# A graph layer on one core: bin counts in PSUM, an earlier rank chain and a new order of the edge phase

## The chip, the cores and the metric

One Trainium2 chip, one core. The metric is the time of the kernel on the device in microseconds (us); where several runs are given, their median. Five engines work side by side: TensorE (PE in the rows, PEld for its weight loads), VectorE (DVE), ScalarE (ACT), GpSimd (POOL) and SyncE (SP, which here issues the plain transfers). Sixteen DMA engines move the data.

## What is computed

A graph layer over 3,327 nodes with 1,024 features, float32. Every node has itself and some 16 others as neighbours (adjacency of int32, density 0.0024 made symmetric, with a full diagonal).

```
h = relu(layernorm(x))
f = h @ Wf + bf
g = h @ Wg + bg
e = relu(f @ g.T)
attention = softmax(where(adj > 0, e, -9e15), axis=1)
out = x + attention @ (h @ W + bW)
```

## The kernel before

The kernel does not form the 3,327 x 3,327 scores. It finds each node's list of neighbours, sorts the nodes by their number of neighbours, and gathers for each node only the rows of its neighbours. (Where a list doesn't fit the layout, a flag sends the kernel to a dense path; with these inputs it isn't taken.) The product A = Wf Wg^T is formed once, so that a node's q = h A + bias and its score with a neighbour is the dot of q with the neighbour's h.

**The loop** (`for i in range(NT - 3)`, 26 tiles of 128 nodes, 23 iterations). SP loads a tile of adjacency, 1.66 MB, into one of five key buffers `r` (`load_adj(i + 5)`, L682, behind the tile that frees the buffer). ScalarE makes ones of the entries and sums them (`degrees`, L699). GpSimd multiplies them by the column number, in two halves (`keys`, L706). VectorE takes the eight largest of each of 16 segments (`segments`, L770 and L772), and out of these 128 candidates the 24 largest as the list (`listed`, L783 to L787; L779 counts the candidates for a later comparison with the degree). Between them stand the layer norm of x (`measured` either on VectorE, L715 and L717, or on ScalarE, L729 and L732; `rooted`, L724, L725 or L733; `inverted`, L737; `scaled`, L742 and L743; `store_h`, L747, to the table `hd` in DRAM), the stores of the lists into the tail of `hd`'s rows (`store_lists`, L757) and of the leftover candidates (`store_left`, L752, into `cd`), and on TensorE the transposes and products that make A (L826, L842, emptied by ScalarE, L846).

**The rank.** Nodes are put in order of their degree, in 48 bins. `one_hot` (L795) marks each node's bin. TensorE sums the one-hots over the nodes ahead: `before(t)` (L803) adds tile t's with an upper triangle, `after(t)` (L806) the rest with a lower one, in one running PSUM tile `pre`; between the two VectorE reads `pre` and keeps each node's place in its bin (`placed`, L811, into `rp`). This alternation goes on through the loop.

**The bridge**, behind the loop: the last tiles are normalised and listed (24 is `late`, 25 is `last`), a scan over the bins (L1040), a multiplication with the one-hots (L1041) and a reduction (L1051) give the rank, L1053 to L1083 turn it into two one-hot matrices (`ohp` by comparison with `iotaq`, a pattern that GpSimd writes, L937), and 26 matmuls (L1087) give `perm`, the order of the nodes (L1101). Then the rows of the first two tiles of the order are gathered from `hd` (L641), transposed, and their q is made in thirds (L1117, emptied at L1137). SP loads the eight parts of W (L996) between the stores.

**The edge phase.** For each of the 26 tiles in the new order: gathers of its own rows (H, `G<-hd,perm`), of the leftovers (C, first tile only) and of each neighbour (G, `G<-hd,G`) on GpSimd (L641), dots on VectorE (`junk`, L1271), the softmax, weighted sums of rows on VectorE (L1324) or on ScalarE and TensorE (L1307, L1311), the next tiles' q on TensorE (L1258), the product with W (L1339), the addition of x by a gather that accumulates, and a scatter. F (L1236 to L1239) makes the first tile's longer list out of the leftovers. All engines run in a static order, which a planner in the file works out when the kernel is built: `steps_of` lists the steps with durations and dependences, `FREE_AT` says when each engine is free to begin, `planned` improves the ranks in `PASSES` rounds with random changes from `SEED`, and the best order found is emitted.

## Time and profile before

| | us |
|---|---|
| median of three runs | 1209.29 (1203.59 to 1210.39) |
| the profiled execution | 1202.4 |
| its span in the trace | 1200.7 |
| TensorE busy | 1092.0 (91%) |
| VectorE busy | 1118.7 (93%) |
| GpSimd busy | 897.1 (75%) |
| ScalarE busy | 606.6 (51%) |

The span is cut in three here: the loop, to about 190 us; the bridge, to about 250; the edge phase, to the end. Busy shares over the whole span mix these three, so the rows below are read by stretch. A timeline row gives the start, the duration, the engine, the line of the code, the operation with its output and inputs, how many there are, and in brackets how long the engine had been idle and who released it.

### The profile page before, as it was taken

How to read it: one execution, taken by the hardware profiler on the slowest of the kernel's cores; microseconds unless marked ns; L12 is line 12 of the kernel's file. 1: busy time of each engine (PE TensorE's matmuls, PEld its weight loads, DVE VectorE, ACT ScalarE, POOL GpSimd, SP SyncE). 2: the span in 40 equal slices, each digit the busy share in tenths (PEclk: the TensorE clock that was granted, in tenths of full speed). 3: DMA queues.
4: the chain of work that ended last, by engine and by line, in shares of the span. 5: the costliest groups of instructions: out<-in, count | busy, mean ns of one | idle time of the engine just before them, and what ended most of it. 6: DMA issues, size and time to landing. Idle time of an engine off the chain costs nothing.

```text
span 1200.7 us, 13971 instructions
## 1 busy us (share of the span) xinstructions
PE 1092.0 (91%) x4508; PEld 696.3 (58%) x4508; DVE 1118.7 (93%) x2209; ACT 606.6 (51%) x925; POOL 897.1 (75%) x627
## 2 busy tenths in 40 slices
PE   2799992699968999999999999999999999999997
PEld 2566661367537567566665666665556656555553
DVE  5999999869998999999999999999999999999982
ACT  6799887427418446535554354444433433333251
POOL 8999999178777888777877788768767777777711
PEclk9799996799988999999999999999999999999999
DMA  9999999699978999997999889889989888898932
GB/s 369 418 406 395 393 376 307 228 346 330 329 228 308 315 310 322 331 327 264 328 330 304 292 282 309 302 269 296 307 280 306 264 287 284 290 309 256 300 105 55
DMA packets 98408, 361.98 MB, mean 301 GB/s; under 512 B 14857, under 2 KB 18184, under 8 KB 95125
## 3 DMA queue, kind: packets, MB, share of 16 engines
q0 software_dynamic: 75264, 274.11, 68.9%
q1 hardware_dynamic: 23060, 86.87, 19.0%
q8 instruction: 37, 0.61, 0.2%
q14 instruction: 47, 0.39, 0.1%
HBM read 331.46 MB, written 29.49 MB: 301 GB/s over the span
## 4 chain that ended last, share of the span: by engine, by line
DVE 37%; PE 28%; DMA 12%; issue 11%; POOL 7%; ACT 4%; SPq 0%; POOLq 0%; DVEq 0%; ACTq 0%
DVE junk L1271 16%; DVE G L1324 13%; PE p_o L1339 11%; PE p_q L1258 8%; PE p_y L1311 6%; DMA G<-hd,G 5%; POOL r L706 4%; DVE cand L772 3%; POOL G L641 2%; PE ps_A L1117 2%; DMA G<-hd,perm 2%; ACT G L1307 2%; DMA A_sb<-in_L_gnn_Wg_dram 1%; DMA hd<-pay 1%; DMA xt<-in_x_dram 1%
## 5 line engine op out<-in xcount | busy, mean ns | idle before, releaser
L641 POOL DMA_INDIRECT G<-hd,G x430 | 557.9, 1297 | 167.5 <-issue 94.5
L1271 DVE CUSTOM_DVE_ANT_0 junk<-G,q 128x1024 uint8<-128x1024 f32 x468 | 562.1, 1222 | 14.3 <-DMA G<-hd,G 9.4
L1339 PE MATMUL p_o<-W_sb,yT 128*128 128x512 f32 x832 | 367.2, 593 | 3.5 <-ACT yT L1335 3.3
L1324 DVE SCALAR_TENSOR_TENSOR G<-G,sc 128x1024 f32<-128x1024 f32 (+1 forms) x281 | 354.4, 1262 | 5.3 <-ACT G L1296 4.3
L1258 PE MATMUL p_q<-A_sb,hT 128*128 128x342 f32 x1152 | 345.6, 451 | 2.0 <-ACT p_q L1267 1.5
L1258 PEld LDWEIGHTS p_q<-A_sb,hT 128*128 128x128 f32 x1152 | 212.9, 190 | 106.7 <-issue 7.4
L1339 PEld LDWEIGHTS p_o<-W_sb,yT 128*128 128x128 f32 x832 | 154.3, 189 | 182.7 <-issue 174.1
L1311 PEld LDWEIGHTS p_y<-ident,G 128*128 128x128 f32 x1552 | 176.2, 142 | 38.4 <-issue 19.6
L1311 PE MATMUL p_y<-ident,G 128*128 128x128 f32 x1552 | 188.9, 275 | 5.3 <-ACT G L1307 3.7
L706 POOL TENSOR_TENSOR r<-r,iotaj 128x1664 f32<-128x1664 f32 (+3 forms) x50 | 183.8, 3718 | 5.0 <-ACT r L699 5.0
L1307 ACT ACTIVATE G<-G,sc 128x1024 f32<-128x1024 f32 x168 | 178.8, 1138 | 0.1
L842 PE MATMUL ps_A<-WgT,WfT 128*128 128x342 f32 x432 | 129.3, 458 | 1.8 <-ACT WfT L837 1.8
L772 DVE MAX8 cand<-r 128x8 f32<-128x208 f32 (+2 forms) x416 | 119.2, 360 | 1.3 <-POOL r L706 1.0
L1264 ACT COPY q<-p_q 128x342 f32<-128x342 f32 x72 | 31.8, 441 | 156.7 <-PE p_q L1258 148.1
L1350 ACT ACTIVATE xp<-p_o,unit 128x512 f32<-128x512 f32 x50 | 34.1, 685 | 142.3 <-PE p_o L1339 116.8
L842 PEld LDWEIGHTS ps_A<-WgT,WfT 128*128 128x128 f32 x432 | 81.1, 191 | 41.7 <-ACT WfT L837 2.0
L699 ACT ACTIVATE r<-r 128x3327 f32<-128x3327 int32 (+3 forms) x27 | 77.3, 2863 | 10.0 <-DMA r<-in_adj_dram 7.2
L1335 ACT COPY yT<-p_y 128x512 f32<-128x512 f32 x52 | 30.1, 585 | 86.3 <-PE p_y L1311 86.0
L641 POOL DMA_INDIRECT xp<-in_x_dram,perm x25 | 46.4, 1856 | 27.0 <-ACT xp L1350 20.0
L1357 POOL DMA_INDIRECT out_dram<-xp,perm x25 | 31.8, 1273 | 40.9 <-DMA xp<-in_x_dram,perm 37.5
L1292 ACT ACTIVATE sc<-sc,unit 128x10 f32<-128x10 f32 (+10 forms) x36 | 11.0, 305 | 78.4 <-DVE unit L1282 51.4
L641 POOL DMA_INDIRECT G<-hd,perm x26 | 36.8, 1417 | 18.2 <-DVE ne L1165 9.3
(149 smaller groups left out, 689.0 us busy)
## 6 DMA issues: line engine op xcount, KB each, us to landing
r<-in_adj_dram SPq DMA_DIRECT2D x24, 1663.5 KB, 11.1
xt<-in_x_dram SPq DMA_DIRECT2D x22, 512.0 KB, 12.2
hd<-xt SPq DMA_DIRECT2D x22, 512.0 KB, 10.6
G<-hd,G POOLq DMA_INDIRECT x430
A_sb<-in_L_gnn_Wg_dram SPq DMA_DIRECT2D x8, 512.0 KB, 17.2
A_sb<-in_L_gnn_Wf_dram SPq DMA_DIRECT2D x8, 512.0 KB, 11.8
W_sb<-in_L_gnn_W_dram SPq DMA_DIRECT2D x8, 512.0 KB, 7.7
cd<-cand SPq DMA_DIRECT2D x25, 64.0 KB, 11.5
```

What stands on the lines that cost most here:

```text
L641: return nc.gpsimd.indirect_dma_start(out=to, out_offset=None, in_=table, in_offset=bass.IndirectOffsetOnAxis(ap=idx, axis=0), **kw,)
L699: nc.scalar.activation(r[:n, b:e], a[:n, b:e], AF.Sign, accum_out=to)
L706: eng.tensor_mul(r[:n, b:e], r[:n, b:e], iotaj[:n, b:e])
L772: nc.vector.max(cands[t][:n, s * 8 : s * 8 + 8], r[:n, s * SW : min(N, (s + 1) * SW)])
L842: nc.tensor.matmul(ps[:, :QB], WfTs[c][:, k, :], WgT[:, k, o : o + QB], start=(k == 0), stop=(k == KD - 1))
L1258: nc.tensor.matmul(ps_q[(3 * t + i) % 2][:, :QB], hT[:, k, :], A_sb[:, k, i * QB : (i + 1) * QB], start=False, stop=(k == KD - 1), skip_gr ...
L1271: nc.vector.tensor_tensor_reduce(junks[k % 2], row(t, k), q[:, :D], 1.0, 0.0, op0=ALU.mult, op1=ALU.add, accum_out=scs[t % 3][:, k : k + 1],)
L1307: nc.scalar.activation(g, g, AF.Copy, scale=scs[t % 3][:, k : k + 1])
L1311: nc.tensor.matmul(ps_y[g][:, c, :], of[:, (4 * g + c) * P : (4 * g + c + 1) * P], ident, is_transpose=True, start=((t, g) not in begun an ...
L1324: nc.vector.scalar_tensor_tensor(y, row_k, scs[t % 3][:, k : k + 1], y, op0=ALU.mult, op1=ALU.add)
L1339: nc.tensor.matmul(ps_o[o], yT[:, k, :], W_sb[:, k, o * CB : (o + 1) * CB], start=False, stop=(k == KD - 1), skip_group_check=True,)
L1350: nc.scalar.activation(to, ps_o[o], AF.Copy, scale=rss[t % 3])
```

## The change

Bin counts. `before`, `after` and `placed` leave the loop. `counted(t)`, for all tiles in one go behind the loop, adds tile t's one-hots into every later tile's 48 columns, in three PSUM banks of ten, ten and six tiles, with a matrix of ones; a tile's own 48 columns get the triangle, and `pre` the total. VectorE then subtracts the banks from the scan, multiplies by the one-hots and reduces: that is the rank.

Order of the bridge. The steps of the rank come first on VectorE; the segments and the list of tile 23 and several measurements come behind `perm`. The two halves of `iotaq` are written once at the start by ScalarE, into the buffers that later hold q, so GpSimd's pattern (L937) goes. The first tile's rows are gathered from x as soon as `perm` is there, and normalised anew; the second tile's still come from `hd`. All parts of W are loaded ahead of that gather, where before two of them came at the end of the bridge.

Check of lists. The count of candidates in `listed` goes; instead the entries of four finished lists are counted at once, and F of the first tile counts its longer list. The matmul that gathers the flag becomes a step of the planner (`ws`).

Planner. New starting times, 40 passes for 30, seed 5 for 3, F longer. All orders of the edge phase are therefore new.

The diff, cut to its core (`...` where lines are left out):

```diff
@@ planner
-PASSES = 30
-SEED = 3
+PASSES = 40
+SEED = 5
-FREE_AT = {"POOL": 238.1, "PE": 266.1, "ACT": 265.3, "DVE": 245.0, "DMA": 238.0}
+FREE_AT = {"POOL": 235.0, "PE": 254.0, "ACT": 253.5, "DVE": 239.0, "DMA": 235.0}
-            add("DVE", 1.8, 1.9, ("F", t), ("Cd", t), frees=[("C", t)])
+            add("DVE", 2.8, 2.9, ("F", t), ("Cd", t), ("Hd", t), frees=[("C", t)])
-                    ("M", t), at=(249.4, 263.2)[t] if t < 2 else 0.0,
+                    ("M", t), at=(240.0, 251.5)[t] if t < 2 else 0.0,
...
@@ listed
-            nc.vector.tensor_scalar(
-                pos[:n], cand[:n], 0.0, None, op0=ALU.is_gt, op1=ALU.add, accum_out=cnt[:n, t : t + 1]
-            )
...
+                some = pos[:n, : (u + 1) * KL]
+                nc.vector.tensor_scalar(some, held[:n, NBIN : NBIN + (u + 1) * KL], 0.0, None, op0=ALU.is_gt)
+                nc.vector.tensor_reduce(
+                    cnt[:n, t - u : t + 1], some.rearrange("p (t k) -> p t k", k=KL), AX.X, ALU.add
+                )
...
+        def counted(t):
+            for b in range(t // RB, -(-NT // RB)):
+                t0, t1 = max(b * RB, t + 1), min((b + 1) * RB, NT)
+                if t1 > t0:
+                    nc.tensor.matmul(
+                        banks[b][:, t0 * NBIN - b * RB * NBIN : (t1 - b * RB) * NBIN], ones,
+                        oh[:, t, None, :].to_broadcast([P, t1 - t0, NBIN]), start=(t == 0), stop=False, skip_group_check=True,
+                    )
+                if b == t // RB:
+                    nc.tensor.matmul(
+                        banks[b][:, (t - b * RB) * NBIN : (t + 1 - b * RB) * NBIN], tri, oh[:, t, :], start=False,
+                        stop=(t + 1 == t1), skip_group_check=True,
+                    )
+            nc.tensor.matmul(pre, ones, oh[:, t, :], start=(t == 0), stop=(t == NT - 1), skip_group_check=True)
...
+            qs = [qpool.tile([P, QW], FP, name="q") for s in ORDER[:2]]
+            HP = P // 2
+            iotaq = [q.bitcast(BF)[:, : HP * NT].rearrange("p (d t) -> p d t", t=NT) for q in qs]
+            for i, to in enumerate(iotaq):
+                nc.scalar.copy(to, iotap[:, i * HP : (i + 1) * HP, None].to_broadcast([P, HP, NT]))
...
@@ behind the loop
             measured(19, True)
             rooted(19)
             inverted(18)
-            s = 0
-            after(counted - 1)
-            for t in range(counted, NT):
-                before(t)
-                segments(NT - 3, s, s + 4)
-                s += 4
-                placed(t)
-                after(t)
...
+            one_hot(last, NT)
+            banks = [p_mm.tile([P, CB], FP, name="ps_A") for _ in range(-(-NT // RB))]
+            for t in range(NT):
+                counted(t)
...
-            nc.vector.tensor_mul(above, oh, incl[:, None, :].to_broadcast([P, NT, NBIN]))
+            for b, ps in enumerate(banks):
+                t0, t1 = b * RB, min((b + 1) * RB, NT)
+                nc.vector.tensor_tensor(
+                    above[:, t0:t1, :], incl[:, None, :].to_broadcast([P, t1 - t0, NBIN]),
+                    ps[:, : (t1 - t0) * NBIN].rearrange("p (t d) -> p t d", d=NBIN), op=ALU.subtract,
+                )
...
-            hps = []
-            for s in ORDER[:2]:
-                hps.append(ln.tile([P, D], FP, name="xt"))
-                gather(hps[-1], hd, perm[:, s : s + 1])
+            load_W(6)
+            load_W(7)
+            hps = [ln.tile([P, D], FP, name="xt")]
+            xs[first] = hps[0]
+            gather(hps[0], x[:, :], perm[:, ORDER[0] : ORDER[0] + 1])
+            measured(late, False)
+            rooted(late)
+            segments(NT - 3, 0, SEG)
+            inverted(late)
+            scaled(late)
+            store_h(late)
+            measured(first, True)
+            rooted(first)
+            measured(last, True)
+            inverted(first)
+            scaled(first)
+            rooted(last)
...
@@ F
+            some, number, due = (G[buf["C", t]][:, i : i + w] for i, w in ((SEG * 8, KX + 8), (D - 2, 1), (D - 1, 1)))
+            nc.vector.tensor_scalar(some, found, 0.0, None, op0=ALU.is_gt, op1=ALU.add, accum_out=number)
+            degree = told(t).bitcast(FP)[:, KL : KL + 1]
+            nc.vector.tensor_scalar(due, degree, 7.0 - KL, 0.0, op0=ALU.add, op1=ALU.max)
+            nc.vector.tensor_tensor(due, due, number, op=ALU.not_equal)
+            nc.vector.tensor_tensor(worst, worst, due, op=ALU.max)
```

The order of the instructions at three places, as the engines get them. VectorE in the loop, before: the count and the list of tile 21, the rank sums, four tiles' one-hots and the segments of tile 22 (`r` are the keys, `cand` the candidates, `held` the lists, `hit,rp` the rank sum).

```order
L779 TENSOR_SCALAR held,cnt<-cand 128x128
L783 MAX held<-cand 128x8
L785 MATCH_REPLACE cand<-held,cand 128x128
L783 MAX held<-cand 128x8
L785 MATCH_REPLACE cand<-held,cand 128x128
L783 MAX held<-cand 128x8
L811 SCALAR_TENSOR_TENSOR hit,rp<-pre,oh 128x48 x2
L795 TENSOR_TENSOR oh<-held,pay 128x192
L772 MAX cand<-r 128x8 x8
L737 RECIPROCAL rstd<-rstd 128x1
L770 TENSOR_TENSOR r<-r,held 128x128
```

Two rank sums and the count stand between one tile's candidates and the next tile's segments.

The same place after.

```order
L779 MAX held<-cand 128x8
L781 MATCH_REPLACE cand<-held,cand 128x128
L779 MAX held<-cand 128x8
L781 MATCH_REPLACE cand<-held,cand 128x128
L779 MAX held<-cand 128x8
L796 TENSOR_TENSOR oh<-held,pay 128x192
L771 MAX cand<-r 128x8 x8
L736 RECIPROCAL rstd<-rstd 128x1
L769 TENSOR_TENSOR r<-r,held 128x128
L771 MAX cand<-r 128x8 x8
```

The count ahead of the list and the two rank sums behind it are gone; one-hots and segments follow the list at once.

VectorE in the bridge up to `perm`, before: the comparison that gives `ohp`, the list of tile 23 with its count, `perm`, and the segments of tile 24 (`tens` is the rank's product in PSUM).

```order
L1083 TENSOR_TENSOR r<-lob,iotaq 128x3328
L737 RECIPROCAL rstd<-rstd 128x1
L737 RECIPROCAL rstd<-rstd 127x1
L779 TENSOR_SCALAR held,cnt<-cand 128x128
L783 MAX held<-cand 128x8
L785 MATCH_REPLACE cand<-held,cand 128x128
L783 MAX held<-cand 128x8
L785 MATCH_REPLACE cand<-held,cand 128x128
L783 MAX held<-cand 128x8
L787 TENSOR_SCALAR pay<-held 128x4x24
L1099 COPY tens<-ps_A 128x26
L1100 SCALAR_TENSOR_TENSOR tens<-ps_A,tens 128x26
```

A whole list stands between `ohp` and `perm`.

The same place after, from the last place product.

```order
L1058 TENSOR_SCALAR r<-r,part_no 128x26x26
L736 RECIPROCAL rstd<-rstd 128x1
L714 BN_STATS st<-r 128x6 x2
L716 BN_AGGR mv<-st 128x2
L714 BN_STATS st<-xt 128x6 x2
L716 BN_AGGR mv<-st 128x2
L1074 COPY tens<-ps_A 128x26
L1075 SCALAR_TENSOR_TENSOR tens<-ps_A,tens 128x26
L1076 TENSOR_SCALAR perm<-tens 128x26
L736 RECIPROCAL rstd<-rstd 128x1 x2
L769 TENSOR_TENSOR r<-r,held 128x128
L771 MAX cand<-r 128x8 x16
```

The list has moved behind `perm`, two measurements stand in its stead, and the segments that follow are those of tile 23, which before stood ahead of the scan.

GpSimd from the last keys to the first neighbours, before (`xt<-hd,perm` is the gather for the first q's, `G<-hd,perm` is H).

```order
L706 TENSOR_TENSOR r<-r,iotaj 127x1663
L937 IOTA iotaq 128x3328
L641 DMA xt<-hd,perm 128x1024 x2
L641 DMA G<-hd,perm 128x1049 x3
L641 DMA G<-cd,perm 128x128
L641 DMA G<-hd,G 128x1024 x26
```

Both gathers for the first q's read `hd`, behind the pattern.

The same place after.

```order
L705 TENSOR_TENSOR r<-r,iotaj 127x1664
L705 TENSOR_TENSOR r<-r,iotaj 127x1663
L641 DMA xt<-in_x_dram,perm 128x1024
L641 DMA xt<-hd,perm 128x1024
L641 DMA G<-hd,perm 128x1049 x3
L641 DMA G<-cd,perm 128x128
L641 DMA G<-hd,G 128x1024 x26
```

The pattern is gone and the first of the two gathers reads x; the gathers behind them are in the same order here.

## Rows read from the trace of the kernel before

**Rows 1.** Windows: each engine's busy us (count), granted clock, DMA share, GB/s.
```profile
50.00:100.00 50.00, 48.99 (x201) 32.99 (x200) 47.47 (x195) 46.40 (x71) 50.00 (x15) 1.00 1.02 409
...
180.00:184.00 4.00, 4.00 (x17) 2.54 (x16) 3.96 (x15) 2.80 (x7) 3.40 (x1) 1.00 1.01 212
...
196.00:200.00 4.00, 0.24 (x2) 0.14 (x2) 2.74 (x11) 3.85 (x9) 4.00 (x2) 0.50 0.91 358
...
300.00:600.00 300.00, 276.85 (x1270) 184.59 (x1269) 289.44 (x449) 145.61 (x212) 233.31 (x174) 0.97 0.90 306
```

**Rows 2.** The chain up to 260 us, in order of time: start, us, what.
```profile
175.54 0.33 SPq L682
175.93 13.63 DMA r<-in_adj_dram
...
227.03 4.19 DMA xt<-hd,perm
```

**Rows 3.** Waits of SP (50:200) and VectorE (180:260, 250:600): total, times, longest.
```profile
SPq L682 <- DVE cand L772: 70.9, 16, 6.5
...
DVE mask L1246 <- DMA G<-hd,perm: 9.6, 3, 6.2
...
DVE junk L1271 <- DMA G<-hd,G: 9.4, 13, 1.7
```

**Rows 4.** Timeline of the loop's last tiles on GpSimd and VectorE.
```profile
165.03 14.75 POOL L706 TENSOR_TENSOR r<-r,iotaj 128x1664 f32<-128x1664 f32 x4 [0.78 <-ACT r L699]
180.59 22.01 POOL L706 TENSOR_TENSOR r<-r,iotaj 128x1664 f32<-128x1664 f32 x6 [0.81 <-ACT r L699]
...
175.51 0.29 DVE L779 TENSOR_SCALAR_CACHE_REDUCE held<-cand 128x128 f32<-128x128 f32 x1
...
177.57 0.19 DVE L811 SCALAR_TENSOR_TENSOR hit<-pre,oh 128x48 f32<-128x48 f32 x1
```

**Rows 5.** Timeline from the loop's end to perm.
```profile
180.99 4.85 PE L842 MATMUL ps_A<-WgT,WfT 128*128 128x342 f32 x16
...
189.67 2.98 ACT L699 ACTIVATE r<-r 127x3327 f32<-127x3327 int32 x1 [2.40 <-DMA r<-in_adj_dram]
...
197.41 0.28 ACT L725 ACTIVATE rstd<-mv,eps 128x1 f32<-128x1 f32 x1
...
200.62 1.04 ACT L729 ACTIVATE lnj<-r 128x1024 bf16<-128x1024 f32 x1
...
203.29 0.29 ACT L733 ACTIVATE rstd<-sums,eps 128x1 f32<-128x1 f32 x1
...
204.76 1.46 DVE L1041 TENSOR_TENSOR r<-oh,incl 128x1248 f32<-128x1248 bf16 x1
...
207.69 1.40 DVE L1051 TENSOR_REDUCE rank<-r 128x26 f32<-128x1248 f32 x1
...
216.25 1.93 PE L1087 MATMUL ps_A<-r 128*128 128x52 bf16 x26 [11.81 <-DVE r L1083]
...
221.52 0.18 DVE L1101 TENSOR_SCALAR perm<-tens 128x26 int32<-128x26 f32 x1
```

**Rows 6.** Timeline of VectorE behind perm: segments, last list.
```profile
221.81 4.51 DVE L772 MAX8 cand<-r 128x8 f32<-128x208 f32 x16
...
235.57 0.18 DVE L787 TENSOR_SCALAR pay<-held 127x24 int32<-127x24 f32 x1
```

**Rows 7.** Timeline of the first gathers, the W loads and the first q.
```profile
227.03 1.11 POOL L641 DMA_INDIRECT xt<-hd,perm  x1 [19.23 <-DVE held L779]
...
237.84 0.85 SPq L996 DMA_DIRECT2D W_sb<-in_L_gnn_W_dram  x2
...
238.73 0.94 POOL L641 DMA_INDIRECT G<-hd,perm  x1 [9.33 <-DVE ne L1165]
...
246.00 0.94 POOL L641 DMA_INDIRECT G<-hd,G  x1 [2.59 <-DMA G<-hd,perm]
...
250.89 0.45 ACT L1137 COPY q<-ps_A 128x342 f32<-128x342 f32 x1 [3.68 <-PE ps_A L1117]
```

More of the change, by code (lines that the diff above doesn't have):

```diff
@@ L607, in rows @@
     def rows(t):
[L608 removed]
+        return min(P, N - t * P) if t < NT else P
     def pieces(t):
@@ L996, in load_W @@
                 nc.sync.dma_start(W_sb[:, k, :], W[k * P : (k + 1) * P, :])
-            late, last = NT - 2, NT - 1
+            late, last, first = NT - 2, NT - 1, NT
             empty()
             load_x(last)
-            for k in range(2):
-                load_W(k)
             one_hot(late, last)
-            one_hot(last, NT)
             measured(19, True)
@@ L1021, in edge_path @@
             store_h(18)
-            scaled(19)
-            store_h(19)
-            load_W(2)
-            measured(20, False)
-            rooted(20)
-            rooted(21)
+            for k in range(2):
+                load_W(k)
             work = kpool.tile([P, N], FP, name="r")
@@ L1072, in edge_path @@
             load_W(4)
-            inverted(23)
-            scaled(23)
-            store_h(23)
-            load_W(5)
-            nc.vector.tensor_scalar(place[:, :, 1, :], ohs, part, None, op0=ALU.mult)
-            measured(last, True)
-            measured(late, False)
-            rooted(late)
-            rooted(last)
             ps = p_mm.tile([P, CB], FP, name="ps_A")
-            nc.vector.tensor_tensor(
-                ohp, lob[:, None, :].to_broadcast([P, P, NT]), iotaq, op=ALU.is_equal
-            )
             for t in range(NT):
@@ L1090, in edge_path @@
                 )
-            inverted(late)
-            scaled(late)
-            store_h(late)
-            inverted(last)
-            scaled(last)
-            store_h(last)
-            listed(NT - 3)
+            measured(21, True)
+            rooted(21)
+            measured(23, True)
+            rooted(23)
             tens = c1.tile([P, NT], FP, name="tens")
@@ L1129, in edge_path @@
             empty()
-            pq.append(bank(0, True))
-            third(pq[0], hTs[0], 0)
+            listed(NT - 3)
+            store_lists(NT - 2 - BATCH, NT - 2)
+            inverted(last)
+            scaled(last)
+            store_h(last)
+            store_left(NT - 3)
+            hps.append(ln.tile([P, D], FP, name="xt"))
+            gather(hps[1], hd, perm[:, ORDER[1] : ORDER[1] + 1])
+            pq.append(bank(0, True))
+            for i in range(3):
+                third(pq[i], hTs[0], i)
+                nc.scalar.copy(qs[0][:, i * QB : (i + 1) * QB], pq[i][:, :QB])
+                if i < 2:
+                    pq.append(bank(i + 1, False))
             transposed(hTs[1], hps[1])
             empty()
-            for j in range(6):
-                if j < 5:
-                    third(pq[j + 1], hTs[(j + 1) // 3], (j + 1) % 3)
-                nc.scalar.copy(qs[j // 3][:, j % 3 * QB : (j % 3 + 1) * QB], pq[j][:, :QB])
-                if j < 2:
-                    pq.append(bank(j + 1, False))
-            store_lists(NT - 2 - BATCH, NT - 2)
-            store_left(NT - 3)
+            for i in range(3):
+                third(pq[3 + i], hTs[1], i)
+                nc.scalar.copy(qs[1][:, i * QB : (i + 1) * QB], pq[3 + i][:, :QB])
             segments(late, 0, SEG)
@@ L1150, in edge_path @@
             store_left(last)
-            for k in range(6, KD):
-                load_W(k)
             over = c1.tile([P, 1], FP, name="over")
```

101 lines of the change are left out of this document (42 added, 59 removed).

## The prediction

> **What bounds the kernel now.** I read the page first, then the loop by windows and waits, then the stretch from the loop's end to the edge phase by the chain and the timeline. VectorE and TensorE are the busiest engines. In the loop that is not the whole story. GpSimd has no gap there (50.00 of 50 us from 50 to 100) and the DMA share stands at 1.02 [rows 1], so a lighter VectorE seems worth nothing. But SP stood on VectorE's segments (L772) for 70.9 us in 16 waits [rows 3]: it loads a tile into a buffer that VectorE has to free. The last load, of tile 25 into tile 20's buffer, goes out at 175.54, as tile 20's segments end, and lands 13.63 us after its start, at 189.56 [rows 2]. GpSimd had tile 20's keys ready before 164.3, where its idle time ahead of 165.03 begins (165.03 and 180.59 start four and six half-tile multiplications, tiles 21, 22 and then 23 to 25 [rows 4]). A tile's segments take 4.8 us (0.28 and 4.51 [rows 6]), so VectorE began tile 20's at 170.7: it lags by 6.4 us. And while the last tile's load runs, the share is still 1.01 but the rate is 212 GB/s, against 409 in the loop [rows 1]: the engines count as busy with little to do.
>
> Behind the loop the bridge is a chain of VectorE, ScalarE and TensorE steps. perm is ready at 221.70, the last list at 235.75, the first gather of the edge phase (H of the first tile) starts at 238.73, the first gather of neighbours at 246.00, the first tile's q is complete at 251.34 [rows 5 to 7]. After that the dots wait for neighbours' rows (9.4 us in 13 waits from 250 to 600 [rows 3]); apart from these VectorE is the bound, with 289.44 of 300 us busy from 300 to 600 [rows 1].
>
> **1, the loop.** Per tile VectorE loses the candidate count (0.29 and its read-out of 0.14, overlapping) and the rank sum (0.19 and 0.08) [rows 4], some 0.6 us; the list check that comes in is two small instructions in four tiles, by like rows 0.45, 0.1 a tile. 0.5 us by some twenty tiles is 10 us, more than the lag of 6.4, so VectorE follows the keys closely at the end and tile 25's load is issued 5 to 6 us earlier. What that does to its landing has two ends: nothing, if the share of 1.02 means a full queue; 6.4, if the load meets free capacity. I take -5.0, since the 212 GB/s row is nearer to the second. All that ScalarE does behind tile 25's degrees moves along: it had waited 2.40 us for that load [rows 5].
>
> **2, the rank.** In the times of before: the last one-hot now stands behind inverted(18), whose input ScalarE finishes at 197.7 [rows 5]. With the shift, 192.7. The 26 tiles' counts are 105 matmuls of 18,096 columns in all, which start when TensorE's last product ends (185.84 in before [rows 5]; 184 here, since the waits for the rank sums go). By the f32 row of 16 matmuls of 342 columns in 4.85 us they take 16.0; by half of what 26 matmuls took at a granted clock of 0.50 (1.93, so 37 ns each) 3.9 [rows 5]. They end at 188 to 200. Wanted are 193.2, and 1.5 us behind it are slack (below), so the cost is 0 to 5.4; I take 0. [...]
>
> Then scan 0.25, subtraction from PSUM in three pieces (1,248 elements, by the 1.46 us multiplication of that size 1.5 to 1.8), multiplication 1.46 and reduction 1.40 [rows 5]: 198.2. The reciprocal for tile 20 stands ahead of the next step. Its input comes from ScalarE, which behind the subtraction (195.1) scales tile 19 (some 1.6) and measures tile 20 in 2.96, as from 200.62 to 203.58 before [rows 5]: 199.6. Then 0.6 for four small steps, 0.85 + 0.86 + 0.38 for the place products, 1.9 for the two halves of the comparison: 204.3. The 26 matmuls (1.93) lie under two measurements of 1.48 on VectorE: 207.3, and **perm at 207.9**, 13.8 us earlier than 221.70. Of these 5.0 are the loop's, 4.8 the segments of tile 23, which now come behind perm, 1.5 a measurement and 2.5 the lists; the rest are waits.
>
> **3, VectorE behind perm.** Segments of tile 23 (4.8, [rows 6]) to 212.7; a wait for ScalarE's measurement of tile 24 to 214.4; measurements of the first and last tile 2.9; lists of 23 with their check 2.7, to 220.1; segments and lists of 24 and 25, by rows 4.8 and 2.1 to 2.4 each, to **233.9** against 235.75 [rows 6]. The stores and the wait that follow took 2.98 us; so **H at 236.9**, 1.8 earlier. Two W loads of 512 KB stood in the queue ahead of it, at 237.84 [rows 7]; in the new program they are issued before the first gather. From H to the first neighbours' gather were 7.27 us; an undisturbed gather landed in 4.19 [rows 2]. I take 5.2, between: **neighbours from 242.1**, 3.9 earlier. The bounds from the two durations are -1.8 and -4.9.
>
> **4, the first q.** The first tile's rows come from x at 208.1 and wait for no store of normalised rows; before, that gather stood 19.23 us and went at 227.03 [rows 7]. Landing 212.3, measured on VectorE to 215.9, scaled at 218.9, then some 19 us for transposes and three thirds of 4.85 (the first at the lower clock): q at 237.9, 13.4 earlier, and the second three thirds of 4.7 and a gather's wait later, at 253.4. This is not what counts: the first dot waits for H's rows (241), the following for the neighbours. VectorE's 9.6 us of waits for these rows [rows 3] also cover the extra 0.9 us of the four new steps in F; without that cover they would cost that.
>
> **5, the edge phase.** The amount of work is the same, but the planner starts from other times, another seed and more passes, so all of the static order is new. Its price does not show in any row of before. VectorE waited 9.4 us for neighbours' rows between 250 and 600, in 13 waits [rows 3]; a new order could save about half, -5, or double them, +9. The planner assumes GpSimd free at 235.0 and TensorE at 254.0; I get 236.9 and about 256, two later each, and an order made for earlier times makes someone wait: +2.
>
> **The sum.** -3.9 + 2 = -1.9 us on the profiled execution's 1202.4, so 1200.5. The median of the runs shown is 1209.29, 6.9 above that execution; against it the forecast is **1207.4 us**. Half a per cent, about what a measurement of this kernel can tell from no change, is 6 us: bounds 1203.2 and 1215.3.
>
> **Rivals.**
> *The order and the early q carry through* (faster). TensorE has made q 13 us earlier and the order is made for that; if the 9.4 us of waits are halved and neighbours come at the early end: -4.9 - 4.7 = -9.6, 1199.7. For it: TensorE and ScalarE enter the edge phase with a lead. Against: VectorE is 96% busy from 300 to 600 and its work is not less. Chance 0.22.
> *The loop ends where it did* (no change). The load of tile 25 lands at 189.56 again, because the queue is full. For it: 1.02. Against: 212 GB/s. Then -3.9 + 5.0 + 2 = +3.1, 1212.4. Chance 0.20.
> *The counts are slow* (slower). TensorE's granted clock was 0.50 from 196 to 200, with TensorE nearly idle [rows 1]. If the counts run at that level and at the 74 ns per 52 columns of the bf16 row, 18,096 columns take 25.8 us and end at 209.8 instead of 194.7: +15.1. It decides as soon as they take over 10.7 us. Sum +13.2, 1222.5. Against: TensorE comes from full work, with products up to 185.84, and works on without a break. Chance 0.07.
> *The order fits badly* (slower). The waits of 250 to 600 double: -3.9 + 9.4 = +5.5, and with neighbours at the late end +7.6, 1214.8 to 1216.9. Chance 0.11.
> The forecast itself (1204 to 1211) has 0.40.
>
> **How the numbers follow.** Faster than 1203.2: nearly all of the first rival and a tenth of the forecast, 0.25. Slower than 1215.3: the slow counts, most of the bad order, and the upper tail of the unmoved loop, 0.17. Within: 0.58. The range leaves out the slow counts and the far ends: 1198 to 1217.
>
> **What would show it.** Step 1: the last adjacency load issued near 170 and landed near 184 or 185. Step 2: matmuls of the counts without gaps, done by 194, perm near 208. Step 3: H near 237, neighbours from 242. Step 4: q near 238 and 253, first dot not waiting for q. Step 5: VectorE's waits from 250 to 600 near 10 us. The forecast is wrong if the last load lands at 189 again, if the counts run past 196, or if VectorE's waits after 300 differ by over 5 us from before.

## The result, and the profile after

The changed kernel takes 1213.07 us in the median of 20 runs, the kernel before, run beside it, 1207.47: a ratio of 1.005, 95% interval 1.0028 to 1.0072. It is half a per cent slower; forecast were 1207.4 against 1209.29, a gain of 1.9. Three of the 20 runs, 1224.44 to 1232.56 us, are slow ones and left out of the ratio, and the profiled execution, 1225.3, is among them, so the rows of the changed kernel come from run e1, the same kernel once more: 1209.2 us, a span of 1207.3, against [rows 1 to 7] with 1200.7. Beside e1 the medians were 1209.21 and 1202.93; the two traced executions, 1209.2 and 1202.4, are about as far apart.

The loop, in the chain and the timeline of e1: the last adjacency load, GpSimd's last keys, and ScalarE's sums of the last tile.

```profile
170.99 0.33 SPq L681
171.38 14.73 DMA r<-in_adj_dram
...
167.94 33.02 POOL L705 TENSOR_TENSOR r<-r,iotaj 128x1663 f32<-128x1663 f32 x9
186.21 2.98 ACT L698 ACTIVATE r<-r 127x3327 f32<-127x3327 int32 x1 [3.08 <-DMA r<-in_adj_dram]
```

The load goes out 4.5 us earlier than in [rows 2] and lands at 186.1, 3.4 earlier. GpSimd's last keys end at 200.96, 1.6 earlier than in [rows 4].

The bridge of e1: the last counts on TensorE, the multiplication and the reduction of the rank, `perm`, the last list, the first gathers.

```profile
187.34 0.18 PE L818 MATMUL pre<-oh,ones 128*128 128x48 bf16 x1
188.68 0.18 PE L809 MATMUL ps_A<-oh,ones 128*128 128x48 bf16 x1 [1.16 <-DVE oh L796]
194.31 0.20 PE L814 MATMUL ps_A<-oh,tri 128*128 128x48 bf16 x1 [5.39 <-DVE oh L796]
196.49 5.79 DVE L1031 TENSOR_TENSOR r<-r,oh 128x1248 f32<-128x1248 f32 x1
202.32 1.45 DVE L1033 TENSOR_REDUCE rank<-r 128x26 f32<-128x1248 f32 x1
211.80 0.18 DVE L1076 TENSOR_SCALAR perm<-tens 128x26 int32<-128x26 f32 x1
238.17 0.18 DVE L783 TENSOR_SCALAR pay<-held 127x24 int32<-127x24 f32 x1
240.89 0.94 POOL L641 DMA_INDIRECT G<-hd,perm  x1 [8.25 <-DVE r L1161]
247.37 1.54 POOL L641 DMA_INDIRECT G<-hd,G  x1 [1.51 <-DMA G<-hd,perm]
```

The counts are no trouble: TensorE waits for the one-hots, not VectorE for the counts. But the multiplication L1031 takes 5.79 us where 1.46 were counted on [rows 5], `perm` comes at 211.98, and the neighbours' gathers begin at 247.37, 1.4 us later than in [rows 7], although the loop ended earlier.

The edge phase by windows (each engine's busy us and count, granted clock, DMA share, GB/s; the third figure pair is VectorE), first the kernel before, which the rows ahead of the prediction didn't show in these stretches:

```profile
180.00:250.00 70.00, 37.24 (x145) 22.74 (x144) 53.11 (x201) 40.30 (x75) 36.13 (x17) 0.73 0.83 281
250.00:350.00 100.00, 94.19 (x403) 60.91 (x403) 94.12 (x153) 43.39 (x63) 78.29 (x59) 0.98 0.90 309
350.00:450.00 100.00, 84.77 (x427) 60.56 (x425) 92.31 (x144) 51.54 (x72) 78.41 (x60) 0.93 0.90 305
450.00:1150.00 700.00, 687.33 (x2802) 429.74 (x2803) 690.20 (x1032) 307.08 (x485) 523.99 (x392) 1.00 0.90 296
```

The same windows of e1:

```profile
180.00:250.00 70.00, 46.27 (x245) 29.07 (x244) 56.28 (x178) 40.41 (x74) 29.10 (x14) 0.83 0.77 260
250.00:350.00 100.00, 79.30 (x341) 52.14 (x340) 88.34 (x150) 40.03 (x57) 80.15 (x59) 0.90 0.89 302
350.00:450.00 100.00, 90.11 (x449) 64.69 (x448) 93.53 (x144) 52.31 (x75) 75.01 (x59) 0.95 0.91 306
450.00:1150.00 700.00, 686.36 (x2792) 431.17 (x2791) 687.34 (x1031) 301.32 (x480) 522.88 (x393) 0.99 0.90 296
```

VectorE's work is nearly the same in both, so its idle time is the account of the difference. Behind 1150 us both idle for 24 us. From 250 to 1150 e1 idles 30.8 us (11.7, 6.5 and 12.7) and the kernel before 23.4 (5.9, 7.7 and 9.8): 7.4 us more. At 250 it was 0.9 us of VectorE's work ahead (902.43 us busy behind that point for 903.35, with 33.22 and 26.72 of them behind 1150). That is the 6.6 us between the spans. TensorE, whose early q was to help, stands 15 us longer from 250 to 350 than before (79.30 of 100 busy for 94.19), and its granted clock there is 0.90. VectorE's largest wait, 250 to 600 (total, times, longest), to be laid beside the 9.4 in 13 of [rows 3]:

```profile
DVE junk L1275 <- DMA G<-hd,G: 13.5, 18, 2.3
```

### The profile page after: what moved, and what is told of

Its sections match the earlier page's. It is cut to its first block, busy times and chain, and to the rows that moved or that the text cites. A ratio compares the mean times of both kernels' runs of the same rounds, so it can differ in the third digit from the quotient of the medians.

```text
span 1223.4 us, 13983 instructions
## 1 busy us (share of the span) xinstructions
PE 1104.6 (90%) x4561; PEld 706.5 (58%) x4561; DVE 1118.3 (91%) x2135; ACT 610.1 (50%) x931; POOL 880.6 (72%) x624
## 3 DMA queue, kind: packets, MB, share of 16 engines
q1 hardware_dynamic: 23060, 86.87, 18.2%
## 4 chain that ended last, share of the span: by engine, by line
PE 51%; POOL 12%; DVE 12%; DMA 11%; issue 8%; ACT 4%; another core or an unknown queue 2%; SPq 0%; POOLq 0%; ACTq 0%; DVEq 0%
PE p_o L1343 20%; PE p_q L1262 18%; PE p_y L1315 9%; POOL r L705 9%; DVE junk L1275 5%; DVE G L1328 4%; DMA G<-hd,perm 4%; DMA G<-hd,G 3%; POOL G L641 2%; DMA r<-in_adj_dram 2%; PE ps_A L1111 2%; DMA A_sb<-in_L_gnn_Wg_dram 2%; PE p_t L1255 1%; ACT G L1311 1%
## 5 line engine op out<-in xcount | busy, mean ns | idle before, releaser
L641 POOL DMA_INDIRECT G<-hd,G x430 | 550.0, 1279 | 196.8 <-issue 93.2
L1262 PEld LDWEIGHTS p_q<-A_sb,hT 128*128 128x128 f32 x1152 | 216.2, 192 | 120.0 <-issue 11.3
L1255 PE MATMUL p_t<-ident,G 128*128 128x128 f32 x192 | 31.9, 304 | 38.1 <-DMA G<-hd,perm 30.6
L641 POOL DMA_INDIRECT xp<-in_x_dram,perm x25 | 43.9, 1756 | 27.0 <-ACT xp L1354 20.0
L1258 ACT COPY hT<-p_t 128x512 f32<-128x512 f32 x48 | 27.5, 587 | 62.6 <-PE p_t L1255 54.6
## 6 DMA issues: line engine op xcount, KB each, us to landing
xt<-in_x_dram SPq DMA_DIRECT2D x22, 512.0 KB, 11.7
```

What stands on the lines that cost most here:

```text
L641: return nc.gpsimd.indirect_dma_start(out=to, out_offset=None, in_=table, in_offset=bass.IndirectOffsetOnAxis(ap=idx, axis=0), **kw,)
L1255: nc.tensor.transpose(ps_t[g][:, k, :], row(t, 0)[:, c * P : (c + 1) * P], ident)
L1262: nc.tensor.matmul(ps_q[(3 * t + i) % 2][:, :QB], hT[:, k, :], A_sb[:, k, i * QB : (i + 1) * QB], start=False, stop=(k == KD - 1), skip_gr ...
```

## The experiments

Each ratio is to the kernel before, run in the same session, with its 95% interval. "Order" is the planner's static order of the edge phase, "light loop" the kernel before with the check of lists moved out of the loop, "new bridge" the changed kernel's.

| run | what | ratio |
|---|---|---|
| e1, e15 | the changed kernel | 1.0057 (1.0035 to 1.008), 1.0069 (1.0043 to 1.0095) |
| e2 | product of the rank from PSUM | 1.0046 (1.0025 to 1.0068) |
| e3 | changed kernel, old planner constants | 1.0134 (1.0094 to 1.0174) |
| e4 | kernel before, new planner constants | 1.0137 (1.01 to 1.0173) |
| e5, e6, e10 | e2, order retimed; seeds 5, 2, 33 (33 with 80 passes) | 1.0045, 1.0076, 1.0104 |
| e16, e17, e18 | the same; seeds 37, 8, 32 | 1.0035, 1.0084, 1.0056 |
| e7, e12 | light loop alone | 0.9968 (0.9948 to 0.9988), 0.9987 (0.9964 to 1.0011) |
| e13 | light loop, order retimed | 0.999 (0.9967 to 1.0013) |
| e9 | light loop, seed 5 | 1.004 (1.0011 to 1.0069) |
| e8, e14 | light loop, seed 6 | 1.0106 (1.0061 to 1.0152), 1.0085 (1.0052 to 1.0119) |
| e11 | e2, first tile measured on ScalarE | 1.0132 (1.0099 to 1.0164) |

**The changed kernel again.**

> The changed kernel unchanged, for a second trace. In its first trace TensorE's work of 250 to 260 us ended at 256.7 to 260.3, but ScalarE and VectorE, which wait for it, went on at 267.2, 274.3 and 277.8 only, while the gathers ran at 400 to 424 GB/s without a pause. Theory 'late signals' (TensorE's signals come late while the gathers fill the DMA engines): the second trace shows such a stretch again between 245 and 280 us, longer or shorter, and the time follows its length: without it 1202 to 1206, with 10 to 15 us of it 1212 to 1222. Rival 'bad order' (the new static order of the edge phase costs 5 to 6 us): no such stretch in a trace near the median of 1213, and the loss lies between 300 and 1150 us.

The loss is there again, 1.0057. In this trace TensorE's matmuls for the second q end at 254.83 us, ScalarE copies their last third at 254.87, and no wait of VectorE from 250 to 1150 is longer than 2.3. In the execution of 1225.3 us, where signals of engines came late between 252 and 278, these matmuls ended at 256.73 and the copy began at 267.20. So here late signals are not what cost the time, and 4.9 of the 7.4 us of additional idle time lie behind 300, as the second theory has it; e1 is the trace to compare.

**Why the multiplication took 5.79 us.** In e2 the differences stay in PSUM, so that the product has one operand there:

```diff
-                    above[:, t0:t1, :], incl[:, None, :].to_broadcast([P, t1 - t0, NBIN]),
-                    ps[:, : (t1 - t0) * NBIN].rearrange("p (t d) -> p t d", d=NBIN), op=ALU.subtract,
+                    own, incl[:, None, :].to_broadcast([P, t1 - t0, NBIN]), own, op=ALU.subtract,
...
-            nc.vector.tensor_mul(above, above, oh)
+                    above[:, t0:t1, :], ps[:, : (t1 - t0) * NBIN].rearrange("p (t d) -> p t d", d=NBIN),
+                    oh[:, t0:t1, :], op=ALU.mult,
```

> The subtraction stays in PSUM and the multiplication with the one-hots reads it there, so that no VectorE step of the rank reads two SBUF operands. In the changed kernel this multiplication took 6.62 us, from 194.90 to 201.52, and GpSimd's last key multiplication ended at 200.20. Theory 'port' (a VectorE step with two SBUF operands waits for GpSimd's running multiplication): the three products take 1.5 to 2.0 us in all beside the same GpSimd work, perm comes 4 to 5 us earlier than 211.2, at 206 to 207, and the first gather of the edge phase 2 to 5 earlier than 240.0. Rival 'form' (this form of multiplication, float32 by bfloat16 in place, is slow by itself): the three products take about 6 us again. The time: 2 to 5 us below the changed kernel if the edge phase takes the earlier start over, no change if the stretch from 245 to 280 swallows it.

The timeline of e2: GpSimd's last keys, the product, the small step behind the reduction, `perm`, the first gathers.

```profile
167.22 33.05 POOL L705 TENSOR_TENSOR r<-r,iotaj 128x1663 f32<-128x1663 f32 x9
194.93 1.57 DVE L1033 TENSOR_TENSOR r<-ps_A,oh 128x480 f32<-128x480 f32 x3
199.65 0.67 DVE L1046 TENSOR_SCALAR ranki<-rank 128x26 int32<-128x26 f32 x1
207.82 0.18 DVE L1081 TENSOR_SCALAR perm<-tens 128x26 int32<-128x26 f32 x1
238.28 0.94 POOL L641 DMA_INDIRECT G<-hd,perm  x1 [7.99 <-DVE r L1166]
244.06 1.54 POOL L641 DMA_INDIRECT G<-hd,G  x1 [0.81 <-DMA G<-hd,perm]
```

GpSimd's keys run until 200.27 as before, and the product beside them takes 1.57 us. So it was not the amount of work: L1031 with both operands in SBUF stood behind GpSimd's multiplications, which ended at 200.96 in e1, and finished 1.32 us behind them. Run e7 (below) shows the same in the old bridge: its multiplication begins 1.06 us before GpSimd's end (200.67), takes 2.38 for 1.46 and ends 1.32 behind. In [rows 4, 5] the keys had ended at 202.6 and the step, of the same form as e7's, began at 204.76. GpSimd was not idle there: it ran its pattern until 207.80, which reads no tile, and the step took 1.46 all the same.

```profile
202.55 5.25 POOL L937 IOTA iotaq<- 128x3328 bf16 x1
```

In e2 `perm` gains 4.0 us, H 2.6, the neighbours 3.3, the end some 1.5 in the median, within the intervals.

The traces of e1 and e7 agree on the wait, with an end 1.32 us behind GpSimd's last keys in both; the prediction had missed it. By what means GpSimd holds VectorE up no run shows.

**The order, exchanged crosswise.** e3 gives the changed kernel the planner constants of the kernel before, e4 the reverse.

```diff
-FREE_AT = {"POOL": 235.0, "PE": 254.0, "ACT": 253.5, "DVE": 239.0, "DMA": 235.0}
+FREE_AT = {"POOL": 238.1, "PE": 266.1, "ACT": 265.3, "DVE": 245.0, "DMA": 238.0}
-PASSES = 40
-SEED = 5
+PASSES = 30
+SEED = 3
-                    ("M", t), at=(240.0, 251.5)[t] if t < 2 else 0.0,
+                    ("M", t), at=(249.4, 263.2)[t] if t < 2 else 0.0,
```

> The changed kernel with the planner's starting times, passes and seed of before (longer F and the step for the flag stay). Theory 'bad order': 4 to 6 us faster than the changed kernel, 1206 to 1209. Theory 'late signals': the first gathers come in the same order, so the stretch from 245 to 280 shows TensorE's signals late again and the time stays at 1209 to 1218.

> The kernel before with the planner's starting times, passes and seed of the changed kernel, all else as before. Theory 'bad order': 4 to 7 us slower than before, 1211 to 1215. Theory 'late signals': within 3 us of before, 1205 to 1211, since the bridge and the first gathers are those of before.

Both exchanges cost more than 1.3%. e3 was to gain 4 to 6 us if the new order was bad, and lost. Its time, 1217.92, is one that late signals would give, but no wait of VectorE in its trace from 250 to 1150 is longer than 4.6 us (9.7 in the execution of 1225.3 us). Each of the two has a large wait of its own among those of VectorE, from 250 to 1150 in e3 and from 245 in e4:

```profile
DVE G L1328 <- ACT G L1300: 12.7, 6, 4.6
DVE junk L1271 <- ACT q L1137: 6.8, 2, 4.9
```

In e3 VectorE waits 12.7 us for rows that ScalarE weights (4.2 in e1). In e4 it waits 6.8 us for the first two q, which the new constants expect at 240.0 and 251.5 and the old bridge completes at 247.7 and 261.5. But each exchange is also a new draw of the order, so what wrong starting times cost by themselves these two runs don't tell.

**The order, made for the right times.** The new constants expect GpSimd free at 235.0, and the trace has it at 240.89 (e2: 238.28). e5 takes e2's kernel and sets all starting times from its trace; e6 and e10 have other seeds.

```diff
-FREE_AT = {"POOL": 235.0, "PE": 254.0, "ACT": 253.5, "DVE": 239.0, "DMA": 235.0}
+FREE_AT = {"POOL": 237.6, "PE": 255.6, "ACT": 254.9, "DVE": 243.0, "DMA": 237.5}
-                    ("M", t), at=(240.0, 251.5)[t] if t < 2 else 0.0,
+                    ("M", t), at=(237.6, 252.8)[t] if t < 2 else 0.0,
```

> The kernel of the second experiment (rank product from PSUM), with the planner's starting times set to what that kernel's own trace shows, each as far below the traced time as the kernel before sets its own (GpSimd 237.6 for 235.0, TensorE 255.6 for 254.0, ScalarE 254.9 for 253.5, VectorE 243.0 for 239.0, first two q 237.6 and 252.8 for 240.0 and 251.5); seed 5 and 40 passes stay. Theory fit (the order was made for a bridge that ends some 3 to 6 us earlier than it does, and VectorE's waits between 310 and 390 us come from that): ratio to the kernel before 0.996 to 1.000, waits of VectorE for neighbours' rows behind 300 us below 6. Theory lot (an order's fit to the chip is a matter of the search's luck, and not of the starting times): anywhere between 0.997 and 1.012, and over 4 us away from the next run, which has the same times and another seed. Theory supply (GpSimd's gathers bound the first 130 us of the edge phase whatever the order): 1.003 to 1.006 in both.

> As the run before, with seed 2 for seed 5: same bridge, same starting times, another order. Theory fit: 0.996 to 1.000 here too. Theory lot: over 4 us from the run with seed 5. Theory supply: 1.003 to 1.006 in both.

e5 is level with e2 (1.0045 and 1.0046): the theory that the order only had wrong starting times falls. e6 is 4.5 us slower by the medians with nothing changed but the seed; the two intervals overlap.

**The loop alone.** e7 is the kernel before with the count of candidates taken out of the loop and the finished lists counted instead; e12 repeats it beside others on another chip.

```diff
-            nc.vector.tensor_scalar(
-                pos[:n], cand[:n], 0.0, None, op0=ALU.is_gt, op1=ALU.add, accum_out=cnt[:n, t : t + 1]
-            )
...
+                some = pos[:n, : (u + 1) * KL]
+                nc.vector.tensor_scalar(some, held[:n, NBIN : NBIN + (u + 1) * KL], 0.0, None, op0=ALU.is_gt)
+                nc.vector.tensor_reduce(
+                    cnt[:n, t - u : t + 1], some.rearrange("p (t k) -> p t k", k=KL), AX.X, ALU.add
+                )
```

> The kernel before with one part of the change alone: no count of candidates in the loop, the entries of four finished lists counted instead (the comparison is against the smaller of degree and list length; the check of the first tile's longer list is left out). Rank sums, bridge and order stay. If a lighter VectorE by itself ends the loop earlier: last adjacency load issued at 170 to 172 and landed at 184.5 to 186 (before 175.54 and 189.56), first gather of neighbours at 241 to 243 (before 246.0). Theory carry: the end moves as much, ratio 0.996 to 0.9975. Theory order (an order is worth its time only at the starting times it was made for, and what comes early waits): ratio 0.999 to 1.004, although neighbours start 3 to 5 us earlier.

> The kernel of run e7 unchanged (the kernel before with the light loop, seed 3), beside the changed kernel and another seed on one chip. If e7's gain is the loop's and no accident of that chip: 0.995 to 0.9985. If it was: 0.9985 to 1.003.

The timeline of e7: the last load, GpSimd's keys, the multiplication of the rank, `perm`, H, the neighbours.

```profile
171.88 0.82 SPq L682 DMA_DIRECT2D r<-in_adj_dram  x2
156.64 44.03 POOL L706 TENSOR_TENSOR r<-r,iotaj 128x1664 f32<-128x1664 f32 x12
199.61 2.38 DVE L1043 TENSOR_TENSOR r<-oh,incl 128x1248 f32<-128x1248 bf16 x1
217.49 0.18 DVE L1103 TENSOR_SCALAR perm<-tens 128x26 int32<-128x26 f32 x1
234.04 0.94 POOL L641 DMA_INDIRECT G<-hd,perm  x1 [9.91 <-DMA hd<-pay]
243.45 0.94 POOL L641 DMA_INDIRECT G<-hd,G  x1 [4.55 <-DMA G<-hd,perm]
```

And its windows, as above:

```profile
180.00:250.00 70.00, 38.74 (x153) 23.79 (x152) 53.78 (x194) 38.32 (x71) 36.73 (x19) 0.76 0.82 280
250.00:350.00 100.00, 91.96 (x391) 58.08 (x389) 95.05 (x149) 42.93 (x63) 77.43 (x60) 0.98 0.91 318
350.00:450.00 100.00, 87.40 (x431) 62.82 (x432) 93.78 (x145) 51.69 (x72) 75.42 (x60) 0.91 0.91 308
450.00:1150.00 700.00, 690.51 (x2810) 430.84 (x2809) 691.17 (x1033) 308.04 (x486) 515.00 (x389) 1.00 0.89 293
```

The small part of the change does what the whole was to do: last load 3.7 us earlier, H 4.7, neighbours 2.5, and the old order, shifted as a whole, still fits (20.0 us of idle VectorE from 250 to 1150 against 23.4). Its H comes at 234.04 with `perm` at 217.67; the changed kernel's at 240.89 with `perm` at 211.98. An early `perm` is not what sets H: the last list on VectorE is, and every list that moves behind `perm` is still ahead of it. H follows the end of the last list by 2.5 us in e1 and e2 and by 2.7 in e7; the rows name the list's store in e7 and the check behind the list in e1 and e2, and which of the two sets H no run separates. In e2, where L1031 is cured and VectorE has no more work from 180 to 250 than in e7 (51.81 us for 53.78), the new bridge idles 18.2 of these 70 us, e7's 16.2:

```profile
180.00:250.00 70.00, 47.70 (x250) 30.62 (x248) 51.81 (x176) 39.66 (x74) 30.80 (x17) 0.83 0.78 270
250.00:350.00 100.00, 81.73 (x354) 52.31 (x353) 91.74 (x154) 39.64 (x57) 78.18 (x58) 0.91 0.91 311
```

On its second chip the light loop was level with the kernel before (0.9987, interval across 1); the gain is 0.1 to 0.3%, clear of noise on one chip only.

**The light loop, order retimed.** All starting times moved to those of e7's trace, seed 3 kept.

```diff
-FREE_AT = {"POOL": 238.1, "PE": 266.1, "ACT": 265.3, "DVE": 245.0, "DMA": 238.0}
+FREE_AT = {"POOL": 233.4, "PE": 259.75, "ACT": 258.95, "DVE": 242.45, "DMA": 233.3}
...
-                    ("M", t), at=(249.4, 263.2)[t] if t < 2 else 0.0,
+                    ("M", t), at=(243.05, 256.85)[t] if t < 2 else 0.0,
```

> Run e7's kernel with the planner's starting times moved to what its own trace shows (GpSimd 233.4 for 238.1, TensorE 259.75 for 266.1, ScalarE 258.95 for 265.3, VectorE 242.45 for 245.0, first two q 243.05 and 256.85, flag 257.5); seed 3 and 30 passes stay. Theory fit (an order made for the right times gains): 0.992 to 0.996, better than run e12. Theory lot (new inputs give a new order, and the old one was uncommonly good): 0.998 to 1.007, worse than run e12.

Between the two theories: a new order, and no better or worse than the old one on the same chip (0.999 and 0.9987).

**Another seed with the old bridge.** Only the planner's random numbers change, with the old bridge and the old starting times (e9: seed 5 and 40 passes).

```diff
-SEED = 3
+SEED = 6
```

> The kernel before with the light loop (run e7), and in the planner seed 6 for seed 3, nothing else: the same bridge, the same starting times, another order of the edge phase. Theory lot (the order of the kernel before is an uncommonly good one, so any other costs some microseconds, whatever the bridge; the new kernel's loss behind 300 us is that): 1.000 to 1.008, that is 0.3 to 1.1 per cent above run e7. Theory bridge (the new bridge itself makes the edge phase longer, by the early q or by the order of the first steps; orders made for the old bridge are all alike): 0.995 to 0.999.

> As the run before with seed 5 and 40 passes, the numbers of the changed kernel. Theory lot: 1.000 to 1.008, and over 3 us away from seed 6 or seed 3. Theory bridge: 0.995 to 0.999.

> Run e8's kernel unchanged (light loop, seed 6), beside seed 3 on the same chip. Theory lot: 1.003 to 1.012, so 0.6 to 1.4 per cent above run e12. If the spread of the seeds came from the other chip on which e8 ran: 0.995 to 0.999, within 0.3 per cent of run e12.

1.0106 and, beside e12 on one chip, 1.0085 against 0.9987: one per cent, some 12 us, for a seed. VectorE's waits for neighbours' rows from 250 to 1150 are here 19.3 us in 22 waits (e14, in whose trace no wait of VectorE there is longer than 2.2), against 7.8 in 13 in e7:

```profile
DVE junk L1274 <- DMA G<-hd,G: 19.3, 22, 2.2
```

Seed 5 gives 1.004. So an order's price is a draw, several times what the light loop gains, and the order of the kernel before was a good draw.

**More orders for the new bridge.**

> The new bridge with the rank product from PSUM and the starting times from its trace (run e5), with seed 33 and 80 passes for seed 5 and 40: a third order for the same bridge. Theory lot: as likely below run e5 as above it, 0.998 to 1.010; that one of the orders for the new bridge comes under 1.000 speaks for it. Theory bridge: 1.003 to 1.008, like runs e5 and e6.

> The new bridge (rank product from PSUM) with the starting times of run e5, seed 37 and 40 passes: a fourth order for the same bridge and times (1.0045, 1.0076 and 1.0104 so far). Theory lot alone (the loss is the draw of the order, and the bridge is as good as the old one with the light loop, whose four orders gave 0.997 to 0.999 twice, 1.004 and 1.009 to 1.011): at least one of these three under 1.002. Theory bridge has its part: all three at 1.003 to 1.011.

> As the run before, with seed 8: a fifth order. Theory lot alone: at least one of the three under 1.002. Theory bridge has its part: all three at 1.003 to 1.011.

> As the two runs before, with seed 32: a sixth order. Theory lot alone: at least one of the three under 1.002. Theory bridge has its part: all three at 1.003 to 1.011.

Six orders made for the new bridge's own times lie from 1.0035 to 1.0104, none under 1.002: by what was set down ahead, this speaks for a part of the bridge itself. It doesn't show one. The four with the old bridge lie from 0.997 to 1.011; the two of them under 1.002 both have seed 3, which the kernel before already had, and the other two, 1.004 and 1.0085 to 1.0106, lie among the six. With spreads that overlap so far, how large the bridge's part is can't be told; e2's two microseconds of idle before 250 are the piece that a trace shows.

**The first tile measured on ScalarE.**

```diff
-            measured(first, True)
+            measured(first, False)
```

Its reciprocal and scaling move behind the list of tile 23.

> The kernel of run e2 (rank product from PSUM, the changed kernel's order) with the first tile's layer norm measured on ScalarE instead of VectorE, so that VectorE doesn't stand behind the gather from x before the last lists (2.11 us of waiting and 1.5 of measuring in e2; 1.2 of waiting comes back). If the last list's end on VectorE sets the first gathers: H at 236 (e2 238.28), first gather of neighbours at 242 (e2 244.06), q as before. Theory carry: the end 1.5 to 2 us earlier than e2, ratio 1.002 to 1.0035. Theory order (what comes early waits in an order made for other times): ratio like e2's, 1.0035 to 1.006.

The bridge did what was expected (H at 236.34, neighbours at 241.61), the end did not: VectorE stood 12.97 us for the second q. TensorE's matmuls for it, ScalarE's copy, VectorE's dot, and the window in which TensorE ended:

```profile
236.34 0.94 POOL L641 DMA_INDIRECT G<-hd,perm  x1 [8.78 <-DVE r L1166]
243.09 14.07 PE L1114 MATMUL ps_A<-A_sb,WfT 128*128 128x342 f32 x48 [0.24 <-issue]
266.22 0.44 ACT L1146 COPY q<-ps_A 128x342 f32<-128x342 f32 x1 [12.94 <-remote]
266.70 1.23 DVE L1280 CUSTOM_DVE_ANT_0 junk<-G,q 128x1024 uint8<-128x1024 f32 x1 [12.97 <-ACT q L1146]
250.00:260.00 10.00, 10.00 (x32) 5.86 (x32) 3.58 (x6) 0.44 (x1) 7.56 (x9) 1.00 1.02 416
```

The matmuls were done at 257.2 and ScalarE's copy of them began at 266.22. The chip was another than that of e2, so neither theory of this run is decided.

**The changed kernel once more.**

> The changed kernel beside run e12 on the same chip. Loop, bridge and order together as before: 1.003 to 1.008, some 0.6 to 1.1 per cent above run e12. If the first comparisons were of that chip only: within 0.3 per cent of run e12.

On the chip of e12 and e14 the changed kernel is at 1.0069, the light loop at 0.9987: the rest of the change costs 0.8%, some 10 us.

## Why the prediction was wrong, by its steps

**Step 1, the loop: right in kind, short in size.** Issued at 170.99 (forecast: near 170), landed at 186.1 (184 or 185), 3.4 us earlier where 5.0 were counted. Of the two ends, 0 and 6.4, the load into free capacity was slightly the nearer. GpSimd's keys ended only 1.6 us earlier, about the two gaps of 0.78 and 0.81 us that [rows 4] show between them. What the loop is worth at the end of the kernel e7 shows on one chip (0.9968); on the other (e12, 0.9987) it is not clear of noise.

**Step 2, the rank: the counts right, the multiplication mis-sized.** TensorE came from full work with a granted clock of 1.00 (180 to 184 us in e1), counted 24 tiles from 179.5 (forecast: 184) to 187.34 and waited for the last two one-hots after that; of the two prices, 16.0 and 3.9, 7.8 lies in between. The slow-counts rival is out.

```profile
180.00:184.00 4.00, 4.00 (x45) 2.75 (x44) 3.79 (x16) 3.13 (x3) 4.00 (x2) 1.00 0.98 263
```

The term that failed is "multiplication 1.46": 5.79 us, because GpSimd's keys still ran. The row [rows 5] it was taken from began at 204.76, after the end of the keys; moving a step earlier moved it beside another engine's work, and the duration didn't come along. The prediction's own figures had the overlap: keys that end 5.0 us earlier than 202.6 end at 197.6, and its multiplication stood at 195.3 to 196.8. `perm` at 211.98 instead of 207.9 is this term: in e2, which cures it, `perm` is ready at 208.00. (The parts that the prediction lists for the 13.8 us of `perm` add up to 13.8; there is no rest left for waits.)

**Step 3, VectorE behind `perm`: right in length, late by step 2.** From `perm` to the last list 26.0 us were forecast; e1 takes 26.4. From H to the neighbours 5.2 were forecast; it was 6.48. Instead of 3.9 us earlier the neighbours came 1.4 later: 4.0 of the 5.3 from H, which came late with `perm`, 1.3 from this gather.

**Step 4, the first q: right, and of little worth,** as it said: q is complete at 240.1 and 255.3 (237.9 and 253.4), the first dot waits for H's rows and not for q, and the next for neighbours' rows.

```profile
246.65 0.25 DVE L1250 TENSOR_SCALAR mask<-iotak,G 128x37 f32<-128x37 f32 x1 [4.33 <-DMA G<-hd,perm]
254.53 1.23 DVE L1275 CUSTOM_DVE_ANT_0 junk<-G,q 128x1024 uint8<-128x1024 f32 x1 [1.18 <-DMA G<-hd,G]
```

**Step 5, the order: the term "+2" failed,** and with it the sum. VectorE's idle time from 250 to 1150 grew by 7.4 us; its waits for neighbours' rows from 250 to 600, which the step had near 10, were 13.5. The bounds of -5 and +9 held it; the value inside was argued from a shift of the starting times by two microseconds, and e5 shows no gain from setting those times right. What the step should have said is that an order is a draw from a search, with a spread of one per cent for the seed alone (e8, e14), that the kernel before holds a good one, with 23.4 us of idle VectorE, and that a new draw is more likely worse: of the twelve other orders in these runs eleven are slower than the kernel before, by 1.0035 and more, and one (e13) is level with it. The 9.4 us of waits [rows 3] alone don't tell a good order: e18 has 8.9 us of them from 250 to 1150, and 1.0056.

**The rivals.** The time is that of "The order fits badly" (1214.8 to 1216.9, chance 0.11): 1.005 of 1209.29 is 1215.3. That the number fits is in part luck. Its sum has the neighbours 1.8 to 3.9 us earlier and the waits doubled to 18.8; what came was neighbours 1.4 us later and waits of 13.5. "The order and the early q carry through" had 0.22 and nothing for it but TensorE's lead, which VectorE's rows don't let through. The two failed terms point the same way, 4.3 us (5.79 for 1.46) and 5.4 (7.4 for 2) to the bad. They don't simply add up, since gathers that start late show again as idle time behind 250: the span grew by 6.6 us where 1.9 less were forecast, a miss of 8.5. The forecast's own 1204 to 1211 had no room for both.

**Left open** are the part of the bridge in the edge phase beside the draw of its order, and what an order has that makes it good on the chip.

## What to carry to other kernels

When a step is moved, its duration is not its own: look at what runs beside it in the new place. Here it was GpSimd's keys beside a VectorE step with two operands in SBUF, 5.79 us where 1.46 were counted; with one operand in PSUM it took 1.57 beside the same keys (e2), and behind their end the old form took 1.46 [rows 5]. A static order that a search has found is a tuned quantity like any other; a change that forces a new draw has to be priced with the spread of draws, some one per cent here, and a small edit that leaves the order and shifts all its engines alike (e7) can be worth more than a large one that gains more ahead of it. And a result that many steps need, like `perm`, is not the end of its chain: here the last list on VectorE was.

## What the runs showed of the hardware

In e1 a VectorE instruction with two SBUF operands that began beside GpSimd's multiplications waited for more than the one that ran: L1031 began at 196.49, GpSimd's nine took 33.02 us, so one ended near 197.3 (an estimate by equal shares), and VectorE still came through only after the last, at 202.28 for 200.96. Short steps with two SBUF operands show no such wait: in e2 the 128x128 step L769 takes 0.27 us beside GpSimd's keys, at 182.87, and alone, at 208.05, and all 26 of these steps in the execution of 1225.3 us take 0.27 to 0.29 us.

```profile
182.87 0.27 DVE L769 TENSOR_TENSOR r<-r,held 128x128 f32<-128x128 f32 x1
208.05 0.27 DVE L769 TENSOR_TENSOR r<-r,held 128x128 f32<-128x128 f32 x1
```

Two steps with one SBUF operand were held as well: in e2 L1046 (128x26) took 0.67 us for the 0.18 of e1 and ended at 200.32, as GpSimd's keys did (200.27). In e7 L1057 (128x26, int32) took 0.79 us for the 0.18 of the kernel before and ended at 205.91, as GpSimd's pattern did (205.87).

In some traces, e9 and e11 on one chip and e12 on another, signals between engines came late while the first gathers ran: VectorE stood 7.70 us for ScalarE up to 277.23 in e9, 12.97 up to 266.70 in e11 and 8.36 up to 278.37 in e12. The chip alone doesn't decide it: in e8 and e10 on the one and e14 and e15 on the other no wait of VectorE from 250 to 280 us is longer than 1.42. e7 and e12 are one kernel on two chips; here is ScalarE's copy of the last third of the second q in e7, and then in e12 that copy, a later one, and VectorE behind it. GB/s from 250 to 260 were 373 and 359.

```profile
258.34 0.44 ACT L1139 COPY q<-ps_A 128x342 f32<-128x342 f32 x1 [4.16 <-PE ps_A L1119]
```

```profile
261.95 0.45 ACT L1139 COPY q<-ps_A 128x342 f32<-128x342 f32 x1 [6.74 <-PE p_q L1205]
276.97 1.07 ACT L1257 COPY hT<-p_t 128x512 f32<-128x512 f32 x2 [5.97 <-remote]
278.37 0.16 DVE L1306 RECIPROCAL unit<-unit 128x1 f32<-128x1 f32 x1 [8.36 <-ACT sc L1295]
```

TensorE's transposes that the copy at 276.97 reads were done at 263.1. VectorE loses 8.4 us there and 3.2 more behind it, the larger part of what lies between e12's profiled execution, 1211.11 us, and e7's, 1195.61. What holds the signals back no run shows.
